# Own-chunk score maxima by row-tiled blocks, masked with half-array products, and new durations in the planner of a two-layer transformer kernel

## The chip, the cores and the metric

The kernel runs on one core of a Trainium2 chip. The metric is the device time of one execution in microseconds (us), as the median of several runs. TensorE is PE in the profile (PEld are its weight loads), VectorE is DVE, ScalarE is ACT, GpSimd is POOL and SyncE is SP.

## What is computed

The input x has 2048 rows (tokens) of 256 numbers. Four stages follow each other, each added to x after a normalization of its result: an attention with 16 heads of 16 numbers whose queries and keys come through low-rank projections and a rotation, a gated feed-forward stage (FFN) with 1024 inner columns and int8 weights, a second attention with ordinary projections, and a second FFN. Cut to what matters here:

```python
x = x + _layernorm(_L0_attn_ref(_layernorm(x), ...))
x = x + _layernorm(_L0_ffn_ref(_layernorm(x), ...))
x = x + _layernorm(_L1_attn_ref(_layernorm(x), ...))
x = x + _layernorm(_L1_ffn_ref(_layernorm(x), ...))
# both attentions, per head
scores = einsum('bhqd,bhkd->bhqk', q, k) * scale
scores = where(key <= query, scores, -inf)
y = einsum('bhqk,bhkd->bhqd', softmax(scores), v)
```

The softmax needs the largest score of each query and head before the exponentials are taken. This kernel computes all scores twice: once with queries on partitions, to find the maxima, and once with keys on partitions, for the exponentials.

## The kernel before

**Tiles.** The tokens are cut into 4 chunks of 512 (CH), a chunk into 4 tiles of 128 (P, TPC). Heads go in groups of four; a group's two pairs are numbered i = 0, 1, and e = 0, 1 says which half of the 128 partitions a head has. Queries and keys are split into a high and a low fp32r part and stacked into 64 rows per head, so a score product uses 64 rows of the array. The two heads of a pair lie in the upper and lower half ("row" tiling, two lanes), and can run beside each other.

**Units.** One unit is a chunk of queries with one group of heads; there are 16 per attention, 32 in all, numbered n. A unit has two parts.

- `maxima` (L660 on) fills PSUM banks with scores, queries on partitions, and DVE reduces each bank to maxima (L701). For the unit's own chunk, which holds the causal diagonal, `diagonal(i)` first writes a mask into two banks with a full-array product of a bf16 identity (L688, 128 rows, "full" tiling), then adds the four diagonal 128x128 scores of each half on top (L693). `block("b")` and `block("c")` compute the remaining scores below the diagonal (L675): tile 3 against 384 keys and tile 1 against 128 in one bank, tile 2 against 256 in another. For older chunks of keys, a block is one product of 512 keys (L675, again) and one reduce. `close()` combines the partial maxima, held in `pml` and `pm`, and negates them into `mx` (L727, L728); PE turns them (L737) and ACT copies them to `mrow` (L741).
- `weighted` runs over the tiles of keys. For each tile and each i it writes the negated maxima into a pair of banks by a product with `sel` (L761), adds the scores (L766), lets ACT take the exponential (L771), and POOL zeroes what lies above the diagonal (L775). A product with V follows (L782): four heads in four column strips of the array ("col" tiling), in fp32, which PE does in two passes.

**PSUM** has 8 banks of 512 fp32 columns. Two pairs at most are held by scores that wait for their exponentials, one bank by the sum of products with V, and the remaining ones by maxima blocks, projections and turns.

**Order.** No engine's order is written by hand. Each step is an `Op` of a `Plan` with an engine, a duration in us, the buffers it reads and writes, a rank (when it is due) and for PE a tiling mode. `Plan.run` plays the engines forward in time: among the operations whose inputs and buffers are there it looks for the one that can start first, takes all of the same engine that could start within NEAR = 0.3 us of it, and issues the one with the lowest rank. A change of tiling counts 0.25 us (SWITCH) and a hop between engines 0.06 (HOP); `lag` is time after an operation during which its result isn't yet usable, 0.2 for PE and none for the others. The durations steer the order alone; the chip takes the time that it takes. There is one plan for each attention (the first with the projections) and one for each FFN.

**FFN.** `front` turns the normalized chunk (L473, L865, L866), 8 pairs of gate and up products follow (L912), and `back` has the down products (L879), a turn (L894) and the addition to x.

Of the kernel before, what the change touches and what calls it, by code (L numbers as in the profile page):

```python
# [30 lines left out]
P = 128  # L31
# [101 lines left out]
class Plan:  # L133
# [3 lines left out]
    HOP, NEAR, SWITCH = 0.06, 0.3, 0.25  # L137

    def __init__(self):
        self.ops = []  # L140

    def op(self, engine, us, fn, r=(), w=(), after=(), hold=(), rank=0.0, mode=None, lanes=(0, 1), lag=0.0):
        bufs = list(dict.fromkeys([*r, *w, *hold]))
        deps = list(after)
        for b in r:
            deps += b.writers
        for b in w:
            deps += b.readers
        o = Op(engine, us, fn, bufs, list(dict.fromkeys(deps)), rank, mode, lanes, lag)
        for b in bufs:  # L150
            b.users.append(o)
        for b in r:
            b.readers.append(o)
        for b in w:
            b.writers.append(o)
        self.ops.append(o)
        return o

    def run(self):
# [9 lines left out]
        while ready:  # L169
            best = []  # L170
            for o in ready:
# [26 lines left out]
                if o.engine == "PE":  # L198
                    at = max([at] + [free.get(("PE", x), 0.0) for x in o.lanes])
                    if o.mode != mode:  # L200
                        at = max([at] + [free.get(("PE", x), 0.0) for x in (0, 1)]) + self.SWITCH
                else:
                    at = max(at, free.get(o.engine, 0.0))
# [3 lines left out]
            at, o = min((p for p in best if p[1].engine == first[1].engine and p[0] <= first[0] + self.NEAR),  # L207
                        key=lambda p: (p[1].rank, p[0]))
# [27 lines left out]
def kernel(ctx: ExitStack, tc: tile.TileContext, x_in, cols_in, rows_in, wd_in, wuq_in, rot_in,  # L236
# [145 lines left out]
    ident16 = const.tile([P, P], BF16, tag="ident16", name="ident16")  # L382
    mask_qk = const.tile([P, TPC, P], BF16, tag="mask", name="mask")

    def make_mask():
        make_identity(nc, ident16)
        nc.gpsimd.memset(mask_qk, 0.0)
        nc.gpsimd.affine_select(out=mask_qk, in_=mask_qk, compare_op=ALU.is_ge, fill=NEG, base=0,
                                pattern=[[0, TPC], [-1, P]], channel_multiplier=1)

    mask_b = setup("POOL", 1.8, make_mask)
# [18 lines left out]
    pms = [const.tile([P, TPC, 2, 2, NCHUNK + 1], F32, tag=f"pm{i}", name=f"pm{i}") for i in range(2)]  # L410

    def make_mx():
        for i in range(2):
            nc.gpsimd.memset(pms[i], NEG)
        for i in range(2):
            nc.gpsimd.memset(mx[i], 0.0)

    mx_b = setup("POOL", 1.6, make_mx)
# [27 lines left out]
    def normalize(plan, dst, src, rs, nm, i, r, w, rank):  # L446
        plan.op("ACT", 0.45, lambda: nc.scalar.activation(dst(), src(), AF.Identity, bias=nm.t[:, i:i + 1],
# [17 lines left out]
    def flipped(plan, src, hold, name, rank):  # L465

        banks = []
        for cc in range(2):
# [6 lines left out]
            plan.op("PE", 0.5, flip, r=[src], w=[s], hold=hold, rank=rank, mode="full", lag=0.2)  # L475
# [3 lines left out]
    def transposed(plan, src, name, rank):  # L479
        dst = wide_buf(f"T_{name}")  # L480
        for cc, s in enumerate(flipped(plan, src, [dst], name, rank)):
            plan.op("ACT", 0.59, lambda cc=cc, s=s: nc.scalar.copy(as_halves(dst.t)[:, cc, :], s.t), r=[s], w=[dst], rank=rank)
# [12 lines left out]
    def stacked(plan, c, what, s, i, bias, hi, lo, rank):  # L495

        plan.op("ACT", 0.69, lambda: nc.scalar.activation(as_halves(hi.t)[:, i, :], s.t, AF.Identity, bias=bias[:, i:i + 1]),
# [51 lines left out]
    def products(plan, s, us, terms, r, hold, rank):  # L549
# [5 lines left out]
        plan.op("PE", us, go, r=r, w=[s], hold=hold, rank=rank, mode="full", lag=0.2)  # L555

    def proj0(plan, c, rank, *dst):
# [23 lines left out]
        for i, (n, a, b) in ((1, (P, DQR, DC)), (0, (DQR, 0, DQR))):  # L581
# [6 lines left out]
            plan.op("PE", 0.5, flip, r=[cd, normed[i]], w=[s], hold=[cT], rank=rank, mode="full", lag=0.2)  # L588
# [56 lines left out]
    def attention(layer, plan, wo, wob, bo, scale):  # L645
        L, KS, Vs, kb, vb = layer.L, layer.K, layer.V, layer.kb, layer.vb
        with tc.tile_pool(name=f"kv{L}", bufs=1) as kv, tc.tile_pool(name=f"at{L}", bufs=1) as at:
# [4 lines left out]
            for tag in ("Q", "y", "pml", "mrow", "pt", "o"):  # L652
# [3 lines left out]
            def maxima(n, c, g, qb):  # L656

                pm, mx_ = Buf(lambda: pms[n % 2], rpm), Buf(lambda: mx[n % 2], rmx)
                pml = new(at, [P, 2, 2, 6], F32, "pml", f"pml{L}{n}", 2)
                full = 2 * (2 * TPC * c + 6)  # L660
# [6 lines left out]
                def block(name, i, e, terms, us, reduces, red_us, kc, dst):  # L667

                    s = bank(f"m{L}{n}{i}{name}{e}")
                    b = 64 * e  # L670
                    rk = rank()

                    def fill():
                        for t, k0, k1, to in terms:
                            nc.tensor.matmul(s.t[:, to:to + k1 - k0], qb.t[b:b + 64, i, t * P:(t + 1) * P],  # L675
                                             KS[kc][b:b + 64, 2 * g + i, k0:k1], start=True, stop=True)

                    plan.op("PE", us, fill, r=[qb, kb[kc][g]], w=[s], hold=[dst], rank=rk, mode="row", lanes=(e,), lag=0.2)
                    plan.op("DVE", red_us, lambda: reduces(s.t), r=[s], w=[dst], rank=rk)

                def diagonal(i):

                    ss = [bank(f"m{L}{n}{i}d{e}") for e in range(2)]
                    rk = rank()

                    def fill():
                        for e in range(2):
                            nc.tensor.matmul(ss[e].t, ident16, mask_qk.rearrange("p t k -> p (t k)"), start=True, stop=False)  # L688
                        for t in range(TPC):
                            for e in range(2):  # L690
                                b = 64 * e
                                at_ = slice(t * P, (t + 1) * P)
                                nc.tensor.matmul(ss[e].t[:, at_], qb.t[b:b + 64, i, at_], KS[c][b:b + 64, 2 * g + i, at_],  # L693
                                                 start=False, stop=t == TPC - 1)

                    plan.op("PE", 1.2, fill, r=[qb, kb[c][g], mask_b, mx_b], w=ss, hold=[pm], rank=rk, mode="row", lag=0.2)
                    for e in range(2):
                        plan.op("DVE", 0.60, lambda e=e: top(pm.t[:, :, e, i, 1], tiles(ss[e].t)), r=[ss[e]], w=[pm], rank=rank())

                def top(dst, src):  # L700
                    nc.vector.tensor_reduce(dst, src, AX.X, ALU.max)  # L701

                def tiles(s):
                    return s.rearrange("p (t k) -> p t k", k=P)

                for i in range(2):
                    diagonal(i)
                    for e in range(2):
                        block("b", i, e, [(3, 0, 3 * P, 0), (1, 0, P, 3 * P)], 0.4,
                              lambda s, i=i, e=e: top(pml.t[:, e, i, 0:4], tiles(s)), 0.60, c, pml)  # L710
                    for e in range(2):
                        block("c", i, e, [(2, 0, 2 * P, 0)], 0.2,
                              lambda s, i=i, e=e: top(pml.t[:, e, i, 4:6], tiles(s[:, 0:2 * P])), 0.37, c, pml)
                    for t in range(TPC):
                        for p in range(c):
                            for e in range(2):
                                block(f"{t}{p}", i, e, [(t, 0, CH, 0)], 0.22,
                                      lambda s, i=i, e=e, t=t, p=p: top(pm.t[:, t, e, i, 2 + p:3 + p], s), 0.60, p, pm)

                def close():  # L720
                    m = mx_.t
                    for t, a, b in ((1, 3, 4), (2, 4, 6), (3, 0, 3)):
                        top(pm.t[:, t, :, :, 0], pml.t[:, :, :, a:b])
                    best = small.tile([P, TPC, 2, 2], F32, tag="top", name=f"top{L}{n}", bufs=4)
                    top(best, pm.t[:, :, :, :, 0:c + 2])
# [6 lines left out]
                plan.op("DVE", 1.05, close, r=[pm, pml], w=[mx_], rank=rk)  # L732
# [7 lines left out]
                plan.op("PE", 0.5, flip, r=[mx_], w=[s], hold=[mrow], rank=rk, mode="full", lag=0.2)  # L740
                plan.op("ACT", 0.59, lambda: nc.scalar.copy(mrow.t, s.t), r=[s], w=[mrow], rank=rk)  # L741
# [356 lines left out]
```

## Time and profile before

| | |
|---|---|
| median of 3 runs | 1487.26 us (1486.95 to 1487.43) |
| profiled execution | 1490.08 us |
| its span, first to last instruction | 1488.4 us |
| mean granted PE clock | 0.935 |
| busy in the span: PE / DVE / ACT / POOL | 1325.1 / 934.5 / 798.0 / 289.6 us |
| first attention, start and rest | 0 to 130, 130 to 624 us |
| first FFN, with projections for the second attention | 680 to 796 us |
| second attention, start and rest | 796 to 830, 830 to 1330 us |
| second FFN | 1373 to 1489 us |

A line of groups gives line, engine, operation, written and read tiles, shape, count, busy time together and mean ns of one, then the idle time before them and who ended it. Busy time of a group counts overlapping instructions once, so where it is less than count times mean, they ran side by side. In a line of the timeline the first number is the start, the second the length of the stretch from first start to last end, and xN the number of records. A matmul's end is modelled and includes the way through the array, so costs are read from the distance of starts.

### The profile page before, as it was taken

The page shows a single profiled execution, that of the slowest core. Times are in us where ns is not written, and L with a number is a line of the kernel's source. Part 1 is how long each engine was busy: PE and PEld are TensorE (multiplying, and loading weights), DVE is VectorE, ACT ScalarE, POOL GpSimd, SP SyncE. Part 2 cuts the span into 40 slices and gives each one's busy share as a digit, 9 for nine tenths or more (in the row PEclk, how much of TensorE's full clock was granted, in tenths as well). Part 3 has the DMA queues.
Part 4 walks back from the last instruction along what each step waited for, and adds up shares of the span by engine and source line. Part 5 has one row for each costly group of instructions (what it writes and reads, how often), then busy time and mean ns, then how long its engine had stood idle before and what let it go on. Part 6 is the DMA issues. An engine that isn't in the chain of part 4 may idle for free.

```text
span 1488.4 us, 22354 instructions
## 1 busy us (share of the span) xinstructions
PE 1325.1 (89%) x8632; PEld 740.4 (50%) x8632; DVE 934.5 (63%) x1932; ACT 798.0 (54%) x1094; POOL 289.6 (19%) x468
## 2 busy tenths in 40 slices
PE   2578999999999999959996999999999999995996
PEld 1344544544454444437764555455444444443875
DVE  1267679678888772424444756886888787333442
ACT  1232664556556668545551345555655666764563
POOL 3010111110001000235631101110000100023564
PEclk9687999899999999969997799999999999997998
DMA  4432230032000000020045023005000000000000
GB/s 148 173 134 90 73 141 28 2 125 75 15 15 1 15 15 16 1 71 0 1 170 212 15 91 122 15 15 183 17 15 15 1 15 15 15 1 1 1 29 29
DMA packets 42618, 78.74 MB, mean 53 GB/s; under 512 B 3891, under 2 KB 8336, under 8 KB 42384
## 3 DMA queue, kind: packets, MB, share of 16 engines
q1 hardware_dynamic: 42080, 75.85, 14.6%
q8 instruction: 67, 1.10, 0.3%
q0 software_dynamic: 144, 1.16, 0.2%
q10 hardware_dynamic: 288, 0.31, 0.1%
q14 instruction: 39, 0.32, 0.1%
HBM read 41.66 MB, written 35.65 MB: 52 GB/s over the span
## 4 chain that ended last, share of the span: by engine, by line
PE 64%; DVE 18%; ACT 6%; DMA 4%; POOL 3%; issue 3%; SPq 1%; POOLq 0%; ACTq 0%; DVEq 0%
PE banks L782 13%; PE banks L761 11%; DVE pm L701 11%; PE banks L675 9%; PE banks L766 8%; PE banks L553 8%; PE banks L912 5%; ACT pt L771 3%; PE banks L693 2%; DVE pml L701 2%; PE banks L688 2%; PE banks L879 2%; DMA Q<-sc_q 2%; PE banks L473 2%; PE banks L795 1%
## 5 line engine op out<-in xcount | busy, mean ns | idle before, releaser
L771 ACT ACTIVATE pt<-banks 128x1024 f32<-128x1024 f32 (+3 forms) x640 | 548.1, 895 | 362.2 <-PE banks L766 332.6
L701 DVE TENSOR_REDUCE pm<-banks 128x1 f32<-128x512 f32 (+1 forms) x896 | 557.8, 682 | 144.0 <-PE banks L675 73.4
L782 PE MATMUL banks<-pt,V 128*32 128x512 f32 (+3 forms) x2560 | 303.5, 545 | 6.7 <-POOL pt L775 6.4
L761 PE MATMUL banks<-mrow,sel 64*128 64x512 f32 (+3 forms) x1280 | 296.3, 429 | 14.6 <-DVE pm L701 5.2
L675 PE MATMUL banks<-K,Q 64*128 64x512 f32 (+3 forms) x1152 | 261.8, 414 | 16.7 <-ACT pt L771 3.5
L775 POOL TENSOR_SCALAR_AFFINE_SELECT pt<-pt 128x256 f32<-128x256 f32 x256 | 104.4, 411 | 870.2 <-ACT pt L771 868.0
L766 PE MATMUL banks<-Q,K 64*128 64x512 f32 (+3 forms) x1280 | 257.8, 373 | 0.0
L761 PEld LDWEIGHTS banks<-mrow,sel 64*128 64x128 f32 x1280 | 139.7, 191 | 197.1 <-ACT pt L771 99.2
L675 PEld LDWEIGHTS banks<-K,Q 64*128 64x128 f32 x1152 | 138.3, 192 | 142.7 <-DVE pm L701 62.1
L701 DVE TENSOR_REDUCE pml<-banks 128x4 f32<-128x512 f32 (+1 forms) x256 | 129.7, 549 | 95.1 <-PE banks L675 94.7
L766 PEld LDWEIGHTS banks<-Q,K 64*128 64x128 f32 x1280 | 143.6, 193 | 7.1
L782 PEld LDWEIGHTS banks<-pt,V 128*32 128x32 f32 x2560 | 52.4, 109 | 101.9 <-issue 76.0
L924 POOL TENSOR_TENSOR fl<-fu,fh 128x512 fp32r<-128x512 f32 x64 | 81.9, 1292 | 79.5 <-ACT fh L923 79.5
L921 DVE SCALAR_TENSOR_TENSOR fu<-banks,cols,sl 128x512 f32<-128x512 f32 x64 | 46.9, 747 | 58.1 <-ACT sl L919 42.0
L693 PE MATMUL banks<-K,Q 64*128 64x128 f32 x512 | 46.9, 307 | 32.1 <-DMA Q<-sc_q 32.1
L912 PE MATMUL banks<-fx,wg 128*128 128x512 f32 x256 | 73.9, 409 | 1.7 <-ACT sl L919 0.9
L912 PE MATMUL banks<-fx,wu 128*128 128x512 f32 x256 | 70.0, 396 | 0.0
L693 PEld LDWEIGHTS banks<-K,Q 64*128 64x128 f32 x512 | 37.5, 207 | 62.6 <-issue 49.8
L923 ACT CAST fh<-fu 128x512 fp32r<-128x512 f32 x64 | 39.5, 620 | 38.4 <-DVE fu L921 38.2
L912 PEld LDWEIGHTS banks<-fx,wg 128*128 128x128 f32 x256 | 48.7, 194 | 14.4 <-DVE fx L866 2.1
L912 PEld LDWEIGHTS banks<-fx,wu 128*128 128x128 f32 x256 | 49.4, 193 | 10.5
L919 ACT ACTIVATE sl<-banks,cols 128x512 f32<-128x512 f32 x64 | 43.1, 687 | 15.2 <-PE banks L912 14.9
(127 smaller groups left out, 1104.5 us busy)
## 6 DMA issues: line engine op xcount, KB each, us to landing
K<-sc_k SPq DMA_DIRECT2D x32, 512.0 KB
Q<-sc_q SPq DMA_DIRECT2D x32, 512.0 KB
sc_k<-kh SPq DMA_DIRECT2D x32, 256.0 KB
sc_k<-kl SPq DMA_DIRECT2D x32, 256.0 KB
sc_q<-qh SPq DMA_DIRECT2D x32, 256.0 KB
sc_q<-ql SPq DMA_DIRECT2D x32, 256.0 KB
x<-in_x_dram SPq DMA_DIRECT2D x4, 512.0 KB
out_dram<-x SPq DMA_DIRECT2D x4, 512.0 KB
```

The lines of the kernel that those rows point to most:

```text
L553: nc.tensor.matmul(s.t[:, at:at + n], a, b, start=start, stop=stop)
L675: nc.tensor.matmul(s.t[:, to:to + k1 - k0], qb.t[b:b + 64, i, t * P:(t + 1) * P], KS[kc][b:b + 64, 2 * g + i, k0:k1], start=True, stop=True)
L693: nc.tensor.matmul(ss[e].t[:, at_], qb.t[b:b + 64, i, at_], KS[c][b:b + 64, 2 * g + i, at_], start=False, stop=t == TPC - 1)
L701: nc.vector.tensor_reduce(dst, src, AX.X, ALU.max)
L761: nc.tensor.matmul(s.t[:, e, 0:nq], sel[b:b + 64, i, :], mrow.t[b:b + 64, off:CH], start=True, stop=False)
L766: nc.tensor.matmul(s.t[:, e, 0:nq], KS[kt // TPC][b:b + 64, 2 * g + i, k * P:(k + 1) * P], qb.t[b:b + 64, i, off:CH], start=False, stop=True)
L771: plan.op("ACT", 0.19 + nq / 620, lambda s=s, pt=pt, nq=nq: nc.scalar.activation(pt.t[:, :, 0:nq], s.t[:, :, 0:nq], AF.Exp, scale=scale), ...
L775: plan.op("POOL", 0.41, lambda pt=pt: nc.gpsimd.affine_select(out=pt.t[:, :, 0:P], in_=pt.t[:, :, 0:P], compare_op=ALU.is_ge, fill=0.0, ba ...
L782: nc.tensor.matmul(av.t[32 * j:32 * j + 32, off:CH], Vs[kt // TPC][:, kt % TPC, DV * h:DV * h + 32], pts[kt, j // 2].t[:, j % 2, 0:nq], st ...
L912: nc.tensor.matmul(s.t[:, i, :], w[:, cc, fc * P:(fc + 1) * P], xT[j].t[:, cc, :], start=n == 0, stop=n == 3)
L921: plan.op("DVE", 0.75, lambda s=s, sl=sl, fu=fu, fc=fc: nc.vector.scalar_tensor_tensor(fu.t, s.t[:, 1, :], col(su_at + fc), sl.t, ALU.mult ...
L924: plan.op("POOL", 1.3, lambda fu=fu, fh=fh, fl=fl: nc.gpsimd.tensor_tensor(fl.t, fu.t, fh.t.bitcast(F32), ALU.subtract), r=[fu, fh], w=[fl ...
```

## The change

Six things change.

1. The own chunk's maxima are computed by blocks of one kind, each in one lane. Block a is query tile 3 against its 512 keys, b is tile 2 against 384 and tile 0 against 128, c is tile 1 against 256. The mask is now written under the diagonal tiles alone, by two products with half of the identity each (`half16`, 64 rows, row tiling) in the lane of the block. `diagonal` and the `pml` tile are gone.
2. Each query tile's maximum over its part of the bank is taken by one reduce of one output column, where one reduce made several before. `close` has one reduce in place of four.
3. The own chunk's blocks of both i come ahead of the older chunks' blocks; before, the older blocks of i = 0 came between.
4. The planner counts 0.14, 0.21 or 0.18 us for a change to row, column or full tiling, and 0.11 (LOAD) for the weight load of a PE operation whose input has just come. The lags are 0.08 for DVE, 0.1 for ACT and 0.2 for PE, and ACT's durations are lower by 0.09.
5. Among the operations that could start soon, each us of waiting counts 0.1 of rank.
6. The FFN's planners look 0.1 us ahead instead of 0.3.

```diff
-    HOP, NEAR, SWITCH = 0.06, 0.3, 0.25
+    HOP, LOAD, SWITCH = 0.06, 0.11, {"row": 0.14, "col": 0.21, "full": 0.18}
+    LAG = {"DVE": 0.08, "ACT": 0.1, "PE": 0.2}
...
-                    at = max([at] + [free.get(("PE", x), 0.0) for x in o.lanes])
-                    if o.mode != mode:
-                        at = max([at] + [free.get(("PE", x), 0.0) for x in (0, 1)]) + self.SWITCH
+                    lanes, more = (o.lanes, 0.0) if o.mode == mode else ((0, 1), self.SWITCH[o.mode])
+                    at = max([at + self.LOAD] + [free.get(("PE", x), 0.0) + more for x in lanes])
...
-                        key=lambda p: (p[1].rank, p[0]))
+                        key=lambda p: (p[1].rank + self.waiting * (p[0] - first[0]), p[0]))
...
     def make_mask():
-        make_identity(nc, ident16)
+        nc.gpsimd.memset(half16, 0.0)
         nc.gpsimd.memset(mask_qk, 0.0)
-        nc.gpsimd.affine_select(out=mask_qk, in_=mask_qk, compare_op=ALU.is_ge, fill=NEG, base=0,
-                                pattern=[[0, TPC], [-1, P]], channel_multiplier=1)
+        for e in range(2):
+            at = half16[64 * e:64 * e + 64]
+            nc.gpsimd.affine_select(out=at, in_=at, compare_op=ALU.not_equal, fill=1.0, base=0,
+                                    pattern=[[64, 2], [-1, P]], channel_multiplier=1)
+            at = mask_qk[64 * e:64 * e + 64]
+            nc.gpsimd.affine_select(out=at, in_=at, compare_op=ALU.is_ge, fill=NEG, base=0,
+                                    pattern=[[64, 2], [0, 2], [-1, P]], channel_multiplier=1)
...
     def make_mx():
-        for i in range(2):
-            nc.gpsimd.memset(pms[i], NEG)
...
+                        def part(t, k0, to, width, start, stop):
+                            nc.tensor.matmul(s.t[:, to:to + width], qb.t[b, i, t * P:(t + 1) * P],
+                                             KS[kc][b, 2 * g + i, k0:k0 + width], start=start, stop=stop)
...
+                        lo = terms[0][3] + terms[0][2] - terms[0][1] - P
+                        for x in range(2):
+                            nc.tensor.matmul(s.t[:, lo:lo + P * len(terms)].rearrange("p (d k) -> p d k", k=P), half16[b, x, :],
+                                             mask_qk[b, x, 0:len(terms), :], start=x == 0, stop=False)
+                        for j, (t, k0, k1, to) in enumerate(reversed(terms)):
+                            part(t, k1 - P, to + k1 - k0 - P, P, False, j == len(terms) - 1)
+                        part(t, k0, to, k1 - k0 - P, True, True)
...
+                    for e in range(2):
+                        block("a", i, e, [(3, 0, CH, 0)], 0.45, c, [(0.6, 3, 0, slice(0, CH))])
+                    for e in range(2):
+                        block("b", i, e, [(2, 0, 3 * P, 0), (0, 0, P, 3 * P)], 0.8, c,
+                              [(0.47, 2, 0, slice(0, 3 * P)), (0.2, 0, 0, slice(3 * P, CH))])
+                    for e in range(2):
+                        block("c", i, e, [(1, 0, 2 * P, 0)], 0.4, c, [(0.34, 1, 0, slice(0, 2 * P))])
...
                 def close():
                     m = mx_.t
-                    for t, a, b in ((1, 3, 4), (2, 4, 6), (3, 0, 3)):
-                        top(pm.t[:, t, :, :, 0], pml.t[:, :, :, a:b])
                     best = small.tile([P, TPC, 2, 2], F32, tag="top", name=f"top{L}{n}", bufs=4)
-                    top(best, pm.t[:, :, :, :, 0:c + 2])
+                    nc.vector.tensor_reduce(best, pm.t[:, :, :, :, 0:c + 1], AX.X, ALU.max)
...
-            plan = Plan()
+            plan = Plan(0.1, 0.1)
```

In the changed kernel the masks have line L690, the blocks L680, the products with `sel` and the scores L755 and L760, and the product with V L776.

## The prediction

> **What bounds the kernel now.** I read the page first (busy shares, chain), then the busy time by stage, then a stretch of the timeline on each engine, then the waits of the weight loads. From the page:
>
> ```profile
> PE 1325.1 (89%) x8632; PEld 740.4 (50%) x8632; DVE 934.5 (63%) x1932; ACT 798.0 (54%) x1094; POOL 289.6 (19%) x468
> PE 64%; DVE 18%; ACT 6%; DMA 4%; POOL 3%; issue 3%; SPq 1%; POOLq 0%; ACTq 0%; DVEq 0%
> ```
>
> TensorE carries the chain, VectorE is second. By stage (us, then busy PE, PEld, DVE, ACT, POOL, clock), the steady parts of the two attentions are
>
> ```profile
> 130.00:624.00 494.00, 480.29 (x3487) 240.45 (x3485) 364.04 (x728) 295.64 (x374) 57.27 (x125) 0.98 0.11 39
> 830.00:1330.00 500.00, 484.40 (x3530) 239.99 (x3528) 360.25 (x698) 298.33 (x369) 56.25 (x126) 0.98 0.11 40
> ```
>
> 994 of 1488 us at almost full clock. PE's 97% is not PE at its peak, since each record includes a pipeline tail. What a product costs is the distance of starts:
>
> ```profile
> 600.25 0.66 PE L693 MATMUL banks<-K,Q 64*128 64x128 f32 x8
> 600.75 0.45 PE L761 MATMUL banks<-mrow,sel 64*128 64x512 f32 x2
> 601.03 0.39 PE L766 MATMUL banks<-Q,K 64*128 64x512 f32 x2
> 601.26 0.39 PE L761 MATMUL banks<-mrow,sel 64*128 64x512 f32 x2
> 601.49 0.40 PE L766 MATMUL banks<-Q,K 64*128 64x512 f32 x2
> 601.82 1.06 PE L782 MATMUL banks<-pt,V 128*32 128x512 f32 x8
> 602.81 0.50 PE L761 MATMUL banks<-mrow,sel 64*128 64x512 f32 x2
> 603.15 0.40 PE L766 MATMUL banks<-Q,K 64*128 64x512 f32 x2
> ```
>
> A pair of 512-column products in the two halves takes 0.23 (601.03 to 601.26). A change of tiling adds 0.10 before L782 (0.33 against 0.23) and, coming back, 0.11 of exposed weight load (602.81 to 603.15, 0.34 against 0.23) besides 0.11 of drain. Eight 128-column products take 0.50, four per half, so 0.11 to 0.12 each, though their columns are a quarter of 0.23: their weight loads bind. Pricing every product of the two steady stages so, in the built program's order, gives 718 us of products and 134 of tiling changes; 138 us are left in which PE stands. Whom its weight loads wait for (total us, times, longest):
>
> ```profile
> PEld banks L761 <- ACT pt L771: 99.2, 138, 1.2
> PEld banks L675 <- DVE pm L701: 62.1, 146, 1.1
> PEld banks L761 <- DVE pm L701: 56.9, 85, 1.4
> PEld banks L675 <- ACT pt L771: 24.4, 54, 0.9
> PEld banks L675 <- DVE pml L701: 19.6, 37, 2.8
> ```
>
> Weight loads also idle while columns stream, so these are upper bounds. I use their ratio, DVE 138.6 to ACT 123.6: about half of the 138 us, 70, is PE at a bank that DVE has not reduced.
>
> **Own-chunk products on PE: 0 us (-4 to +3).** There are 64 pairs of unit and i. Before: mask and diagonal 1.03 (599.71 to 600.75, one change of tiling inside), block b 0.28 to 0.34, c 0.12 behind others: 1.45. After, per half: a is mask 128, mask 128, 128, 384; b is mask 256, mask 256, 128, 128, 256; c is mask 128, mask 128, 128, 128. The columns per half stay 2304, the matmuls of one i rise from 16 to 26. With 0.11 wherever an f32 load follows a short product, and 0.23 per 512 columns otherwise: a 0.44, b 0.56, c 0.39, sum 1.39. No row shows a bf16 load of 64 rows; the nearest is L688's, 101 ns against 207 for L693's. At the f32 price the sum is 1.49.
>
> That assumes that the halves overlap, though a half's four or five matmuls now stand in a row ahead of the other's. The Trainium skill speaks against it ("TensorE: Matmul & The Clock Gate", The mechanism, in Part 3): matmuls start strictly in program order and only weight loads are pulled ahead. By that rule only a half's last matmul overlaps: an i costs about 2.4 and the sum is +61 us. Block b tests the rule: its program order is 384 and 128 in one half, then 384 and 128 in the other. In a stretch without waits, and over the whole run:
>
> ```profile
> L675 PE MATMUL banks<-K,Q 64*128 64x384 f32 x2 | 0.4, 438 | 0.0
> ...
> L675 PE MATMUL banks<-K,Q 64*128 64x384 f32 x128 | 39.2, 442 | 1.7 <-DVE pm L701 0.8 <-DVE ql L499 0.5
> ```
>
> Two of 438 ns cover 0.4 us together: they ran side by side, so the second overtook the 128 between. 128 x 442 is 56.6 us and covers 39.2. The trace decides: a half runs ahead. How far is open: in row tiling at most two matmuls are overtaken, in L782's four column tiles three (all four first passes start within 20 ns). Blocks a and c need three, b four. If b's second half starts late, by its two masks, that is 0.23 x 64 = +15 us. I take full overlap and keep +15 for the range.
>
> **Tiling changes: -4 us.** The masks were full-array products among row-tiled ones; now they are row-tiled. By the two orders PE changes tiling 851 times before and 774 after (full to row 132 to 85, row to full 97 to 75, column to full 37 to 16, the pairs with columns almost unchanged). At 0.10 to row from full, 0.21 or 0.22 from row, 0.13 from column (the usual excess of starts over products in the trace) that is 142 to 131.5; 6 of the 11 are inside the 1.03 above.
>
> **VectorE: 0.**
>
> ```profile
> 133.03 0.41 DVE L701 TENSOR_REDUCE pml<-banks 128x2 f32<-128x256 f32 x1
> 133.36 4.86 DVE L701 TENSOR_REDUCE pm<-banks 128x1 f32<-128x512 f32 x8
> 138.14 0.29 DVE L701 TENSOR_REDUCE pm<-pml 128x4 f32<-128x4 f32 x3
> 138.47 0.20 DVE L701 TENSOR_REDUCE top<-pm 128x16 f32<-128x48 f32 x1
> ```
>
> By starts a 512 reduce takes 0.60 (4.78/8) and a 256 one 0.33, so 384 takes 0.47 and 128 0.20. Own chunk per half and i: 0.60+0.60+0.33 = 1.53 before, 0.60+0.47+0.20+0.33 = 1.60 after, +0.28 a unit; the three small reduces of the close go, -0.33. Over 32 units -2 us, off the path: DVE is busy 74% and 72% of the steady stages.
>
> **The planner: -18 us (-42 to +10).** Nothing else in its edit computes; it reorders. I compare the orders. *Bursts:* a maxima block needs a bank until DVE has read it. Runs of maxima blocks with no other PE work between, longer than four banks, hold 258 us of reduces before and 178 after, 31% less. If DVE's half of the stalls shrinks with it, 0.31 x 70 = -21. It can be won because DVE has a quarter idle. *Exponentials:* between the last score of a key tile and its L782 stand on average 4.5 us of PE work before, 4.2 after; under 2.4 us (two exponentials of 1.02 and the hops) 9 of 224 full tiles before, 18 after. What is missing there grows by 7 us at most; ACT is mostly ahead, so +2. *Starts:* each attention now issues nearly three units' own blocks before its first score, in runs of up to 25 banks at DVE's pace: +3 (0 to 6). *FFN:* its planner looks 0.1 instead of 0.3 ahead. Before, a turn stands between products and waits:
>
> ```profile
> 690.56 0.30 PE L894 MATMUL banks<-ident,yT 128*128 128x128 f32 x1
> 691.59 0.98 PE L894 MATMUL banks<-ident,yT 128*128 128x128 f32 x7 [0.73 <-ACT yT L885]
> ```
>
> After, 24 gate and up products cover the first such wait of each layer: two times about 1 us, -2. ACT's lower durations change no instruction.
>
> **Hidden.** POOL's new masks (selects of two at 0.41 and two at 0.65 instead of 0.29 and 0.65, a memset of half16, none for pm) add about 1 us after 10.5; POOL then sits idle for 5.55 us until wk_raw lands at 22.2, so 0; without that cover, +1. SP's queue keeps its DMAs; a few loads of Q and K move by one to six places. The long waits for Q (12.1 and 12.3) are at the attentions' starts, where SP's order is as before: 0, at most one landing of 9 us.
>
> **Sum.** 0 - 4 + 0 - 18 = -22 against the profiled execution's 1490.1 (span 1488.4 and 1.7 around it): 1468. The median of the runs is 2.8 lower, so 1465.
>
> **Rivals.** (1) *All stalls shrink:* ACT's half by the same 31% too, and none of the debits: -4 - 43 = 1440. For it: tiling changes, lags and load times planned before (0.25 each, no lag for DVE) are far from the 0.10 to 0.22 in the rows. Against: exponentials come nearer to their users. 0.17. (2) *The order is worth nothing,* stalls move elsewhere: ACT and DVE are both 60 to 75% busy and banks are eight. 1487 - 4 + up to 4: 1483 to 1489, centre 1486. 0.10. (3) *Slower: the halves don't overlap in the new blocks.* Place: L680 and L690, 64 times; price 0.95 each, 61 us: 1465 + 61 = 1526. It decides once the extra time of an i passes 22/64 = 0.34 us, more than b alone can cost (0.23), so a or c must fail as well. Block b's overtaking speaks against it, their greater depth for it. With milder forms, where half of it meets a worse order, 0.16. The forecast itself, 1450 to 1482: 0.57.
>
> 0.2% (3 us) is about what a measurement of this kernel tells from no change. Faster: 0.57 + 0.17 + 0.03 of (2) = 0.77; same 0.07; slower 0.16. The range 1437 to 1492 leaves out most of (3) and the tail of (1).
>
> **What would show it.** Right: L690 and L680 at row tiling with two records of a size covering little more than one; PEld's waits on DVE for maxima and scores down by some 30%; about 774 tiling changes; DVE's busy time within 5 us of 934; steady stages near 485 us each. Wrong: records of L680 of one size covering twice their mean; waits of L776 for ACT up by more than 7 us; DVE's waits moved to the starts of the attentions.

## The result and the profile after

The changed kernel takes 1462.83 us (median of 4 runs, 1461.8 to 1463.44), the kernel before 1487.11 (4 runs). The ratio is 0.9839, with an interval of 0.9822 to 0.9856: 24 us or 1.6% faster. The profiled execution took 1462.36, its span is 1460.6, the mean granted PE clock 0.935 as before.

The page of the kernel after, its busy line and its chain:

```profile
PE 1315.2 (90%) x9272; PEld 764.7 (52%) x9272; DVE 927.6 (64%) x1964; ACT 795.5 (54%) x1094; POOL 290.6 (20%) x468
PE 64%; DVE 17%; ACT 6%; DMA 3%; issue 2%; POOL 2%; SPq 0%; POOLq 0%; ACTq 0%; DVEq 0%
```

PE has 640 matmuls more and is busy 10 us less. The engines' shares of the chain have hardly moved, so the page alone does not tell where 24 us went. The steady parts of the two attentions, now 8 and 12 us shorter (columns as before: stretch, length, busy PE, PEld, DVE, ACT, POOL, clock, DMA share, GB/s):

```profile
130.00:616.00 486.00, 475.51 (x3706) 249.33 (x3705) 361.97 (x739) 294.58 (x371) 56.78 (x123) 0.98 0.12 40
818.00:1306.00 488.00, 480.49 (x3802) 250.53 (x3801) 362.54 (x724) 297.75 (x369) 55.49 (x124) 0.97 0.12 41
```

The same pricing by distances of starts as in the prediction gives an estimate for the two stages together (130 to 616.5 and 818 to 1306 after):

| us | before | after | |
|---|---|---|---|
| products in row tiling | 378.0 | 404.4 | +26.4 |
| products in full tiling | 113.0 | 89.3 | -23.7 |
| products in column tiling | 227.4 | 225.9 | -1.5 |
| changes of tiling | 134.0 | 123.9 | -10.1 |
| PE stands | 138.2 | 125.1 | -13.1 |
| sum | 990.6 | 968.6 | -22.0 |

By this estimate the masks moved from full to row tiling at little cost (26.4 against 23.7), the changes of tiling give 10, and 13 come from stalls. The sum of the rows is measured; how it is shared among them depends on the prices taken. Over the whole run, with the cuts at each attention's first score and each FFN's first gate and up product, the lengths fall by 7.4 (first attention), 4.5 (first FFN up to the next attention's first score), 12.1 (second attention) and 3.7 us (second FFN). That is 27.7 together, about 3 more than the medians give, since the profiled execution of the kernel before was itself 3.0 above its median.

The new own-chunk blocks, one i of one unit in a stretch without waits inside it (timeline of PE):

```profile
828.56 0.27 PE L690 MATMUL banks<-mask,half 64*128 64x128 bf16 x3 [0.25 <-DVE pm L698]
828.64 0.30 PE L680 MATMUL banks<-K,Q 64*128 64x128 f32 x1
828.65 0.22 PE L690 MATMUL banks<-mask,half 64*128 64x128 bf16 x1
828.68 0.53 PE L680 MATMUL banks<-K,Q 64*128 64x128 f32 x3
829.02 0.41 PE L690 MATMUL banks<-mask,half 64*128 64x256 bf16 x3
...
829.59 0.28 PE L690 MATMUL banks<-mask,half 64*128 64x128 bf16 x2
...
830.16 0.64 PE L776 MATMUL banks<-pt,V 128*32 128x256 f32 x8
```

By program order block a's first half would issue two masks, a 128 and a 384 before the second half's first mask. The trace has three masks first and only then the first f32 product: the third mask belongs to the other half. From 828.56 to the next kind of work at 830.16 the i takes 1.60, with the change to column tiling (0.21) in it. Groups of the same two lines by shape, over the whole run:

```profile
L680 PE MATMUL banks<-K,Q 64*128 64x384 f32 x128 | 39.7, 427 | 0.0
...
L690 PE MATMUL banks<-mask,half 64*128 64x128 bf16 x512 | 57.6, 233 | 3.8 <-DVE pm L698 3.2 <-ACT pt L765 0.2
```

128 x 427 is 54.7 us and covers 39.7; 512 x 233 is 119.3 and covers 57.6. Whom PE's weight loads wait for (us, times, longest):

```profile
PEld banks L755 <- ACT pt L765: 101.1, 159, 1.2
PEld banks L680 <- DVE pm L698: 76.2, 171, 0.9
...
PEld banks L755 <- DVE pm L698: 59.3, 108, 1.5
...
PEld banks L680 <- ACT pt L765: 12.9, 24, 1.0
```

The waits on DVE are 135.5, against 138.6 before; those on ACT 114.0 against 123.6. One line of the kernel before is not in the 138.6:

```profile
PEld banks L761 <- DVE pml L701: 6.4, 14, 0.8
```

With it the fall is from 145.0 to 135.5, or 7%. The fall by a third that the prediction wanted on DVE's side is not there, although the total came out.

### The profile page after: what moved, and what is told of

Its sections match the earlier page's. It is cut to its first block, busy times and chain, and to the rows that moved or that the text cites. A ratio compares the mean times of both kernels' runs of the same rounds, so it can differ in the third digit from the quotient of the medians.

```text
span 1460.6 us, 23690 instructions
## 1 busy us (share of the span) xinstructions
PE 1315.2 (90%) x9272; PEld 764.7 (52%) x9272; DVE 927.6 (64%) x1964; ACT 795.5 (54%) x1094; POOL 290.6 (20%) x468
## 4 chain that ended last, share of the span: by engine, by line
PE 64%; DVE 17%; ACT 6%; DMA 3%; issue 2%; POOL 2%; SPq 0%; POOLq 0%; ACTq 0%; DVEq 0%
PE banks L776 14%; DVE pm L698 12%; PE banks L755 11%; PE banks L680 10%; PE banks L760 7%; PE banks L558 7%; PE banks L906 6%; ACT pt L765 3%; PE banks L690 2%; PE banks L873 2%; PE banks L478 2%; DMA sc_q<-ql 1%; PE banks L789 1%; DMA Q<-sc_q 1%; PE banks L731 1%
## 5 line engine op out<-in xcount | busy, mean ns | idle before, releaser
L698 DVE TENSOR_REDUCE pm<-banks 128x1 f32<-128x512 f32 (+3 forms) x1280 | 687.0, 602 | 209.0 <-PE banks L680 200.7
L680 PE MATMUL banks<-K,Q 64*128 64x512 f32 (+3 forms) x1664 | 331.3, 394 | 37.2 <-DMA Q<-sc_q 31.5
L776 PE MATMUL banks<-pt,V 128*32 128x512 f32 (+3 forms) x2560 | 300.6, 544 | 2.7 <-POOL pt L769 2.2
L755 PE MATMUL banks<-mrow,sel 64*128 64x512 f32 (+3 forms) x1280 | 286.6, 425 | 13.8 <-ACT mrow L735 4.6
L680 PEld LDWEIGHTS banks<-K,Q 64*128 64x128 f32 x1664 | 196.6, 201 | 143.1 <-DVE pm L698 76.2
L760 PE MATMUL banks<-Q,K 64*128 64x512 f32 (+3 forms) x1280 | 251.3, 372 | 0.0
L755 PEld LDWEIGHTS banks<-mrow,sel 64*128 64x128 f32 x1280 | 134.6, 190 | 198.4 <-ACT pt L765 101.1
L760 PEld LDWEIGHTS banks<-Q,K 64*128 64x128 f32 x1280 | 135.9, 192 | 6.7
L776 PEld LDWEIGHTS banks<-pt,V 128*32 128x32 f32 x2560 | 52.5, 109 | 90.7 <-issue 73.7
L690 PE MATMUL banks<-mask,half 64*128 64x128 bf16 (+1 forms) x768 | 95.1, 254 | 4.9 <-DVE pm L698 3.8
L690 PEld LDWEIGHTS <-half 64*128 64x128 bf16 x768 | 43.3, 98 | 50.8 <-issue 47.5
L906 PEld LDWEIGHTS banks<-fx,wg 128*128 128x128 f32 x256 | 48.3, 193 | 12.8 <-DVE fx L860 2.3
L735 ACT CAST mrow<-banks 128x512 fp32r<-128x512 f32 x32 | 18.8, 587 | 60.2 <-PE banks L731 60.1
```

What stands on the lines that cost most here:

```text
L680: nc.tensor.matmul(s.t[:, to:to + width], qb.t[b, i, t * P:(t + 1) * P], KS[kc][b, 2 * g + i, k0:k0 + width], start=start, stop=stop)
L690: nc.tensor.matmul(s.t[:, lo:lo + P * len(terms)].rearrange("p (d k) -> p d k", k=P), half16[b, x, :], mask_qk[b, x, 0:len(terms), :], sta ...
L698: plan.op("DVE", red_us, lambda t=t, p=p, src=src: nc.vector.tensor_reduce(pm.t[:, t, e, i, p:p + 1], s.t[:, src], AX.X, ALU.max), r=[s], ...
L755: nc.tensor.matmul(s.t[:, e, 0:nq], sel[b:b + 64, i, :], mrow.t[b:b + 64, off:CH], start=True, stop=False)
L760: nc.tensor.matmul(s.t[:, e, 0:nq], KS[kt // TPC][b:b + 64, 2 * g + i, k * P:(k + 1) * P], qb.t[b:b + 64, i, off:CH], start=False, stop=True)
L776: nc.tensor.matmul(av.t[32 * j:32 * j + 32, off:CH], Vs[kt // TPC][:, kt % TPC, DV * h:DV * h + 32], pts[kt, j // 2].t[:, j % 2, 0:nq], st ...
```

## Where the stalls still are

One stretch of the kernel after shows PE waiting for DVE most plainly (PE's timeline, first attention, unit 10):

```profile
439.07 1.06 PE L776 MATMUL banks<-pt,V 128*32 128x512 f32 x8
440.07 10.53 PE L680 MATMUL banks<-K,Q 64*128 64x512 f32 x18
450.41 0.37 PE L690 MATMUL banks<-mask,half 64*128 64x128 bf16 x2
450.54 0.88 PE L680 MATMUL banks<-K,Q 64*128 64x128 f32 x2
...
455.27 1.11 PE L731 MATMUL banks<-ident,mx 128*128 128x128 f32 x4 [0.27 <-DVE pm L698]
```

Between the product with V at 439.07 and the turn at 455.27 PE does nothing but 25 maxima blocks: the first 18 in 10.5 us, 0.58 each, where in pairs they cost about 0.12 each. That is DVE's pace, 0.60 a reduce. Its weight loads show it one by one (start, length, and in brackets the wait):

```profile
443.24 0.18 PEld L680 LDWEIGHTS banks<-K,Q 64*128 64x128 f32 x1 [0.41 <-DVE pm L698]
443.84 0.18 PEld L680 LDWEIGHTS banks<-K,Q 64*128 64x128 f32 x1 [0.42 <-DVE pm L698]
444.43 0.28 PEld L680 LDWEIGHTS banks<-K,Q 64*128 64x128 f32 x1 [0.41 <-DVE pm L698]
445.03 0.28 PEld L680 LDWEIGHTS banks<-K,Q 64*128 64x128 f32 x1 [0.32 <-DVE pm L698]
```

Every 0.60 us one load, and ahead of each a wait for the reduce that frees its bank. By the distances of starts PE stands for 11.2 of the 15.2 us. The busy time in slices of 10 us (kernel after) suggests why it isn't given back:

```profile
440.00:450.00 10.00, 9.32 (x22) 4.21 (x19) 10.00 (x18) 1.11 (x3) 2.35 (x1) 0.71 0.00 0
450.00:460.00 10.00, 9.73 (x60) 7.92 (x60) 9.48 (x22) 1.61 (x2) 0.00 (x0) 0.50 0.01 2
460.00:470.00 10.00, 9.92 (x75) 4.99 (x72) 2.78 (x7) 8.28 (x9) 0.00 (x0) 0.94 0.00 0
470.00:480.00 10.00, 10.00 (x82) 4.04 (x82) 0.01 (x1) 9.46 (x11) 1.44 (x4) 1.00 0.01 2
```

First DVE is full and ACT empty (1.11, 1.61), then ACT full and DVE empty (2.78, 0.01). Two engines that could work side by side work one after the other. PE's record is "busy" 9.32 in the first slice with 22 matmuls; only their number tells that it stands. The planner plays the banks and DVE forward, so it issues block after block as each bank comes free; that it prefers them to scores here was read from its order, and which term of its choice does it was not traced.

## Experiments

Three theories stand in the expectations. A: the two parts of the change, new blocks and planner, add, and the planner's part comes from its measured prices. B: the blocks bring nearly all, or the lags alone do. C: any new order moves the time by up to 10 us, whatever the prices. Later a fourth, D: what separates the orders is whether a long run of maxima blocks like the one at 440 stands in them; each bank beyond the first four costs 0.6 less PE's own 0.13, so 0.47 us. The runs come from three chips: the first four experiments from one where the kernel before took 1485.87 us, four (the FFN's look ahead, either half of the prices, the price of waiting) from one with 1485.18, the others from one with 1487.28. Between chips the ratios are what to compare; 0.001 of ratio is 1.5 us. Parts 1 to 3 of the change were only run together.

**The blocks alone.** The changed kernel with the planner, durations and lags of before.

```diff
-    HOP, LOAD, SWITCH = 0.06, 0.11, {"row": 0.14, "col": 0.21, "full": 0.18}
-    LAG = {"DVE": 0.08, "ACT": 0.1, "PE": 0.2}
+    HOP, NEAR, SWITCH = 0.06, 0.3, 0.25
...
-            plan = Plan(0.1, 0.1)
+            plan = Plan()
```

> The new own-chunk blocks, masks, reduces and close with the planner of before (one price of 0.25 for every change of tiling, no load time, lag for PE alone, ACT's durations as before, 0.3 us ahead everywhere). Theory A (two parts add up: blocks save tiling changes, 851 to about 775, the planner saves the rest): 1487 - 7 = 1480, 1476 to 1484. Theory B (the blocks are the whole gain, the planner's numbers only reshuffle): 1463 to 1467. Theory C (any new order moves the time by some 10 us either way, luck): anywhere from 1470 to 1500.

**The planner alone.** The kernel before with parts 4 to 6 of the change; the planner's durations of scores (nq/1110) and of older blocks (0.233) are the changed kernel's too.

```diff
-    HOP, NEAR, SWITCH = 0.06, 0.3, 0.25
+    HOP, LOAD, SWITCH = 0.06, 0.11, {"row": 0.14, "col": 0.21, "full": 0.18}
+    LAG = {"DVE": 0.08, "ACT": 0.1, "PE": 0.2}
...
-                        key=lambda p: (p[1].rank, p[0]))
+                        key=lambda p: (p[1].rank + self.waiting * (p[0] - first[0]), p[0]))
...
-            plan = Plan()
+            plan = Plan(0.1, 0.1)
```

> The own-chunk maxima as before with the new planner (its prices, load time, lags, ACT durations, price of waiting, 0.1 us ahead in the FFNs). Theory A: 1487 - 18 = 1469, 1464 to 1474. Theory B: 1483 to 1490. Theory C: anywhere from 1465 to 1495.

Blocks alone: 1480.83 (ratio 0.9964, 0.9952 to 0.9976), -5.0 against 1485.87 on the same chip. Planner alone: 1466.52 (0.9869, 0.9855 to 0.9882), -19.4. Together -24.4, and the whole change gave -24.3. The parts add, so the first half of A holds and B's first form falls. The orders of other runs below scatter by several us, so that the sum fits to 0.1 us is partly chance. In the kernel with the blocks alone the weight loads wait so:

```profile
PEld banks L755 <- ACT pt L765: 126.1, 191, 1.2
PEld banks L755 <- DVE pm L698: 70.0, 114, 1.2
PEld banks L680 <- DVE pm L698: 44.4, 114, 0.8
PEld banks L680 <- ACT pt L765: 22.7, 49, 0.8
```

On DVE 114.4, on ACT 148.8: DVE's waits are 21 us shorter than in the kernel after, which is 18 us faster. The sum by engine doesn't rank these orders.

**How far the planner looks,** 0.2 and 0.4 us instead of 0.3.

```diff
-    def __init__(self, near=0.3, waiting=0.1):
+    def __init__(self, near=0.2, waiting=0.1):
```

> The changed kernel with the attentions' planner looking 0.2 instead of 0.3 us ahead; no duration differs. Theory A: within 4 us of 1463, since what it takes for the durations is unchanged. Theory C (luck of the order): 5 to 15 us away, most likely slower, as 1463 would be a lucky draw.

```diff
-    def __init__(self, near=0.3, waiting=0.1):
+    def __init__(self, near=0.4, waiting=0.1):
```

> The changed kernel with the attentions' planner looking 0.4 instead of 0.3 us ahead. Theory A: within 4 us of 1463. Theory C: 5 to 15 us away, most likely slower.

0.2: 1480.68 (0.9972, 0.9963 to 0.9981). 0.4: 1464.7 (0.9858, 0.9843 to 0.9874). A number that says nothing of the chip moves the time by 18 us (20 by the ratios, 0.9972 against 0.9839), more than the 5 to 15 of C; 0.4 stays within A's 4 us. So part of C is right. At 0.2 the first attention is 12.8 us longer than in the kernel after, the second 6.6. It has runs of 28 banks at 317 (15.3 us) and 18 at 858 (8.9 us); 0.4 has one of 29 at 310 (17.7 us). So the runs account for some of it, not for the distance between these two.

**The FFN's look ahead as before.**

```diff
-            plan = Plan(0.1, 0.1)
+            plan = Plan()
```

> The changed kernel with the FFNs' planner looking 0.3 us ahead again. The two FFNs with what follows them were 8 us shorter in the changed kernel's trace. Theory A (the shorter look ahead is what covered the turns): 1463 + 6 = 1469, 1466 to 1472. Theory B (the durations did it): 1463 to 1465. In either case both attentions keep their length within 2 us.

1464.26 (1463.27 to 1468.84; ratio 0.9859, 0.9842 to 0.9875), 1.4 more than the kernel after by the medians and 3 by the ratios, and the intervals overlap. B had said 1463 to 1465, A 1466 to 1472. Its profiled execution was the slowest of its four, so its stages are not compared one by one. In the traces the second FFN takes 115.0 us before and in the kernel with the blocks alone, both with 0.3, 117.8 in this one, and 110.9 to 113.3 in all those with 0.1. The wait at the first turn is gone in the kernel after (timeline of PE):

```profile
688.77 1.07 PE L906 MATMUL banks<-fx,wu 128*128 128x512 f32 x4
...
689.68 1.03 PE L888 MATMUL banks<-ident,yT 128*128 128x128 f32 x8
```

Before, the turn stood 0.73 for ACT in the midst of its eight products; now gate and up products fill that place. The traces speak for 2 to 4 us per FFN, the medians and ratios for 1.4 to 3 in all, which is within the noise. The share of the look ahead is not settled.

**The two halves of the prices.** Tiling and load prices as before, lags and durations new; then the reverse; then both as before.

```diff
-    HOP, LOAD, SWITCH = 0.06, 0.11, {"row": 0.14, "col": 0.21, "full": 0.18}
+    HOP, LOAD, SWITCH = 0.06, 0.0, {"row": 0.25, "col": 0.25, "full": 0.25}
```

> The changed kernel with a change of tiling at 0.25 for all and no load time in the planner; lags and the rest stay. Theory A (the prices of tiling and load are the planner's gain): 1473 to 1480. Theory B (the lags are): 1462 to 1466. Theory C (the order is luck): anywhere up to 1485.

```diff
-    LAG = {"DVE": 0.08, "ACT": 0.1, "PE": 0.2}
+    LAG = {"DVE": 0.0, "ACT": 0.0, "PE": 0.2}
...
-        o = Op(engine, us, fn, bufs, list(dict.fromkeys(deps)), rank, mode, lanes, lag or self.LAG.get(engine, 0.0))
+        o = Op(engine, us + (0.09 if engine == "ACT" and us != 1.9 else 0.0), fn, bufs, list(dict.fromkeys(deps)), rank, mode, lanes, lag or self.LAG.get(engine, 0.0))
```

> The changed kernel with no lag for DVE and ACT in the planner and ACT's durations longer by 0.09 as before; prices of tiling and load stay. Theory A (the prices of tiling and load are the gain): 1462 to 1467. Theory B (the lags are): 1470 to 1480, with the weight loads' waits on DVE longer by 10 us or more. Theory C: anywhere up to 1485.

The third has both edits.

> The changed kernel with both undone in the planner: 0.25 for every change of tiling and no load time, and no lag for DVE and ACT with ACT's durations 0.09 longer. Its order has two long runs of maxima blocks in the second attention, 22 and 36 banks. Theory D (a run of maxima blocks goes at DVE's pace and costs PE about 0.47 us a bank over the first four; the other orders of the new planner are worth about 1452): 1452 + 0.47 x 50 = 1475, 1468 to 1482. Theory A (the prices are the gain): no further than the 1481 of the old planner, and it would be there without such runs, so 1495 to 1505 with them.

Old tiling prices 1465.66 (0.9873, 0.9858 to 0.9888), old lags 1460.17 (0.9839, 0.9818 to 0.986), both old 1507.68 (1.0134, 1.0118 to 1.015). Each half alone keeps the gain to within about 5 us, without both it is lost and the kernel is slower than before. So neither guess about a single half came true: A had put the old tiling prices at 1473 to 1480, B the old lags at 1470 to 1480. The last has two runs of maxima blocks, 23 banks at 959 us and 37 at 974, 35.5 us together. Unit 21, where the second of them lies, takes 56.6 us from its first score to the next unit's, about 28 more than in most other orders. As an estimate, without these 28 us it would stand near 1480, where the blocks alone stand. That would be A's picture of prices with D's accident on top, but it isn't shown: D alone had said 1468 to 1482, A with such runs 1495 to 1505, and 1507.68 lies above both. Why either half is enough isn't settled.

**The price of waiting off** (part 5 of the change undone in the attentions; the FFNs keep it).

```diff
-    def __init__(self, near=0.3, waiting=0.1):
+    def __init__(self, near=0.3, waiting=0.0):
```

> The changed kernel with the price of waiting (0.1 of rank per us) at 0 in the attentions; the FFNs keep it. Within a look ahead of 0.3 us it is worth 0.03 of rank, about one step of a unit with 36 to 60 steps. Theory A: within 3 us of 1463. Theory C (the order is luck, as the 18 us between a look ahead of 0.2 and 0.3 would say): 5 us or more away.

1452.82 (0.9785, 0.977 to 0.9799), 10 us less than the kernel after by the medians, 8 by the ratios, where A had allowed 3. It has no such run at 440 (the same slices):

```profile
440.00:450.00 10.00, 9.64 (x67) 4.45 (x67) 8.68 (x15) 7.05 (x9) 2.38 (x1) 1.00 0.01 2
450.00:460.00 10.00, 10.00 (x89) 5.04 (x86) 7.75 (x17) 7.92 (x9) 0.00 (x0) 1.00 0.00 0
```

DVE and ACT work beside each other, 67 and 89 matmuls instead of 22 and 60. From its first score to the next unit's, unit 10 takes 50.8 us here and 63.0 in the kernel after. The price of waiting, then, isn't what brought the gain; in this order it cost. From this came D, and two more orders, whose runs of blocks could be read from the programs beforehand: with 0.25 two runs of 52 banks and two of 25 (the trace has 53 and 26), with 0.4 none.

```diff
-    def __init__(self, near=0.3, waiting=0.1):
+    def __init__(self, near=0.25, waiting=0.0):
```

> The changed kernel, attentions planned 0.25 us ahead and without a price of waiting. Durations as in the changed kernel. Its order has runs of 25 and 52 banks of maxima in each attention. Theory D: 1452 + 0.47 x (21 + 48) x 2 = 1517, 1490 to 1525, with DVE at 100% and PE's clock down to half in these runs. Theory C (orders scatter by some 10 us without a nameable place): 1450 to 1480.

```diff
-    def __init__(self, near=0.3, waiting=0.1):
+    def __init__(self, near=0.4, waiting=0.0):
```

> The changed kernel, attentions planned 0.4 us ahead and without a price of waiting. Its order has no run of over 13 banks of maxima, and 13 only at the start of the second attention. Theory D: 1450, 1445 to 1456. Theory C: 1455 to 1480.

0.25: 1523.24 (1.0238, 1.022 to 1.0257), within D's 1490 to 1525. PE's timeline of it:

```profile
461.86 27.90 PE L680 MATMUL banks<-K,Q 64*128 64x128 f32 x49
490.76 0.79 PE L755 MATMUL banks<-mrow,sel 64*128 64x512 f32 x2 [1.00 <-DVE pm L698]
```

and its slices:

```profile
460.00:470.00 10.00, 10.00 (x38) 6.30 (x35) 10.00 (x22) 0.42 (x1) 0.00 (x0) 0.50 0.00 1
470.00:480.00 10.00, 10.00 (x19) 4.67 (x18) 10.00 (x18) 0.00 (x0) 0.00 (x0) 0.50 0.00 0
```

In these 20 us ACT is busy for 0.42. The two units that hold the runs take 90.8 and 90.2 us where the order before this one has 50.8 for each, about 0.5 us for each of their 79 banks. They lose 79 us together, the whole run some 68 (1.0238 against 0.9785): other units give some of it back.

0.4: 1465.84 (0.985, 0.9832 to 0.9868), where D said 1450 and C 1455 to 1480. It has no long run, and yet is 13 us slower than with 0.3 (10 by the ratios). The loss lies before the first FFN, which starts at 660.0 us against 646.1; the second attention is as long in both. It is spread over the first attention: its first unit is 5.7 us longer, five others 1.5 to 3.2, and no single run of blocks carries it. D explains the large losses, not the scatter of about 7 us either way that is left between orders.

**The blocks' durations from the trace.** The change guessed 0.45, 0.8 and 0.4 for a, b and c; the trace of the kernel after has 0.47, 0.58 and 0.35 for a pair. The new order's longest runs are two of 18 banks (9.5 us at 141, 8.0 at 838).

```diff
-                        block("a", i, e, [(3, 0, CH, 0)], 0.45, c, [(0.6, 3, 0, slice(0, CH))])
+                        block("a", i, e, [(3, 0, CH, 0)], 0.47, c, [(0.6, 3, 0, slice(0, CH))])
...
-                        block("b", i, e, [(2, 0, 3 * P, 0), (0, 0, P, 3 * P)], 0.8, c,
+                        block("b", i, e, [(2, 0, 3 * P, 0), (0, 0, P, 3 * P)], 0.58, c,
...
-                        block("c", i, e, [(1, 0, 2 * P, 0)], 0.4, c, [(0.34, 1, 0, slice(0, 2 * P))])
+                        block("c", i, e, [(1, 0, 2 * P, 0)], 0.36, c, [(0.34, 1, 0, slice(0, 2 * P))])
```

> The changed kernel with the planner's durations of the new blocks as the changed kernel's trace has them for a pair of halves: a 0.47, b 0.58, c 0.36 in place of 0.45, 0.8, 0.4. Its order has lost the run of 24 banks at 440 us. Theory D: 1463 - 0.47 x 20 = 1453, 1448 to 1458. Theory C: 1455 to 1480.

1450.84 (5 runs, 1448.67 to 1453.98; ratio 0.9754, 0.9735 to 0.9772): the fastest of all, 12 us under the kernel after, and where D put it (1448 to 1458). Unit 10 takes 49.0 us. Its slices at the same place:

```profile
440.00:450.00 10.00, 9.64 (x65) 4.55 (x63) 8.40 (x20) 5.94 (x8) 2.77 (x3) 1.00 0.00 1
450.00:460.00 10.00, 9.98 (x76) 4.19 (x72) 7.49 (x13) 6.84 (x7) 0.88 (x1) 1.00 0.01 2
```

That measured durations are better in general isn't shown by this; one order without a long run came of them.

## Why the prediction was right, and where its steps were not

**Own-chunk products, 0 (-4 to +3): right.** From a pair of blocks to the next start, lower quartile, a takes 0.47, b 0.58, c 0.35, sum 1.40 (predicted 0.44, 0.56, 0.39, 1.39). In the table the three kinds of product rise by 1.2 together. The Trainium skill's rule ("TensorE: Matmul & The Clock Gate", The mechanism, in Part 3), that matmuls start strictly in program order, with its +61, is contradicted by the trace for two halves of the array, and rival (3) falls: in most pairs the second half's first mask starts at most 66 to 69 ns (a and c) or 127 ns (b) after the first half's, with up to three matmuls of the other half overtaken. The +15 kept for b came to little: b is 0.02 over its estimate, 1.3 us for 64 pairs.

**Tiling changes, -4: direction right, size off.** The table has -10.1, nearly the whole of the 11 that were priced. The prediction took 6 of them off as already inside the old 1.03; but products as such rose by only 1.2, so nothing stands against those 6. The traces count 851 changes of tiling before and 774 after, as forecast, 765 with the blocks alone and 852 with the planner alone: the saving comes from the blocks. The blocks alone gave only -5.0 as a whole; what their order lost again under the old planner was not traced.

**VectorE, 0: not contradicted.** DVE is busy 927.6 against 934.5, -6.9 where -2 was said, and outside the 5 us that the prediction allowed; with the blocks alone it is 932.4, so -2.1. DVE holds 17% of the chain after and 18% before, so it is not off the path altogether; what its 6.9 us were worth there is not shown.

**The planner, -18: the total right, the bursts' mechanism not.** The planner's part measured -19.4 alone and -19.3 on top of the blocks. The step that failed is "if DVE's half of the stalls shrinks with it, 0.31 x 70 = -21": the waits on DVE fell by 3 us of the 139 that it used, or by 9.5 of 145 with the line left out, not by 31%. The static sum counted the reduces in runs over four banks and treated a run of 25 like five of 5; a run's banks beyond the fourth each cost, and in the kernel after one run of 25 holds 11.2 us of stalls at 440. By the table stalls fell by 13.1 in the steady stages, where -21 and +2 were said; an order without that run, as the last experiment has, stands 12 us lower. That the whole, -22 said and -24.3 measured, came so close is therefore partly luck: by the table the stalls gave less than was said and the tiling changes more, and other look-aheads and durations in the same planner gave anything from 1451 to 1523 us. What made up the -19.4 of the planner alone was not priced. *Exponentials, +2:* waits on ACT fell by 9.6 and no new ones appeared at L776. *Starts, +3:* the length up to the first attention's first score is 98.4 against 98.5, so 0 there; the second attention's start lies within the -4.5 of the stretch before it, where a small loss could not be told apart. Behind its first score, its first three units take 73.8 us against 69.9, with runs of 18 and 17 banks among them. *FFN, -2:* 1.4 to 3 in all by the medians and ratios, within the noise, and some 2 to 4 per FFN by the traces.

**Hidden, 0: right**, as far as the same start of 98.4 shows.

**Rivals.** (2), that the order is worth nothing, falls by the second experiment. (1), that all stalls shrink by 31%, did not happen here, though the order at 1451 has come about half of the way from 1463 to 1440.

Two things stay open: why either half of the prices suffices, and what in the order makes the scatter of some 7 us among orders without long runs. The sums of waits by engine don't rank them.

## What to carry to other kernels

Of an order made by a planner, look at the single longest stretch in which one engine's work stands alone, not only at a sum over bursts: here its cost grew by about 0.5 us with every bank beyond those that were free, and a slice where one consumer is full and the other empty shows it. When a planner's constants are changed, run several neighbours of them before a gain or a loss is put down to the constant: here 0.2, 0.3 and 0.4 gave 1481, 1463 and 1465. Products in two halves of the array can be written half after half: with four or five matmuls of one half in a row they still overlapped here.

## What was not expected of the hardware

The granted clock of PE falls to 0.50 in a run at DVE's pace, although PE has a matmul every 0.60 us in it: 0.71 and 0.50 in the slices at 440 and 450 of the kernel after (the loads above lengthen from 0.18 to 0.28 us at 444.4), 0.50 through 450 to 490 in the kernel with the runs of 53, 1.00 in the same slices of the fastest kernel. The Trainium skill ("TensorE: Matmul & The Clock Gate", A second HAM failure mode) tells of a PE that is throttled by frequent short pauses between groups of matmuls; here one product in one half of the array per 0.60 us was little enough. In the run the loads still start every 0.60 us after the clock has fallen (444.43 and 445.03 above), so the pace stays DVE's; what follows begins with the half clock: from 456 to 460, after the run, it is still 0.50.

In one half, the bf16 masks over 64 rows start some 66 ns apart for 128 columns, where an f32 product of the same shape is followed after 0.11 to 0.14 us, and their weight loads take 98 ns against 201 for the f32 ones.
